# Context attention: queries projected in two parts behind two score groups, all other array shapes behind the third, and a last key block projected with 96 other rows

## The chip, the core and the metric

The kernel runs on one core of a Trainium2 chip. The core has five engines that run their own instruction queues in order: TensorE (PE, with a weight-load half PEld), VectorE (DVE), ScalarE (ACT), GpSimd (POOL) and SyncE (SP), whose queue issues nearly all DMAs here. They wait for each other through semaphores. The metric is the device time of one execution in microseconds (us); the time of a kernel is the median of several executions.

## What is computed

One transformer block in float32 on x of shape (2, 1024, 256), with a context of shape (2, 154, 192): self attention, attention to the context, and a gated feed-forward, each behind a layer norm and with a residual.

```python
def _attention(xq, xkv, wq, wk, wv, wo, bo):        # 16 heads of 64
    q = (xq @ wq).reshape(B, S, N_HEADS, D_HEAD)
    k = (xkv @ wk).reshape(B, T, N_HEADS, D_HEAD)
    v = (xkv @ wv).reshape(B, T, N_HEADS, D_HEAD)
    attn = softmax(einsum('bihd,bjhd->bhij', q, k) * D_HEAD ** -0.5, axis=-1)
    return einsum('bhij,bjhd->bihd', attn, v).reshape(B, S, D_ATTN) @ wo + bo

x = _attention(h1, h1, sa_wq, sa_wk, sa_wv, sa_wo, sa_bo) + x        # h1 = layernorm(x)
x = _attention(h2, cond_emb, ca_wq, ca_wk, ca_wv, ca_wo, ca_bo) + x  # h2 = layernorm(x), 154 keys
a, gate = split(layernorm(x) @ ff_w1 + ff_b1)
x = a * gelu(gate) @ ff_w2 + ff_b2 + x
```

## The kernel before

Work is cut into 16 *units*: 2 batches times 8 pairs of heads (128 columns of the projections). The program is written out by hand in order (`manual_schedule`): each engine runs its instructions in the order in which the Python code emits them, and the framework adds the semaphore waits. Three stages follow each other: self attention (about 0 to 719 us), context attention (about 719 to 948) and feed-forward (to the end).

*Self attention* has 128 steps `p` of two score tiles each (L465). VectorE takes the row maxima (L626), ScalarE the exponentials (L476), and four small DMAs exchange the halves' statistics (`exchange`, L486). One step later `join` (L490 to L503) computes a correction: POOL forms `dd`, ScalarE `ee` (L498), POOL `zz` and `den`; VectorE a reciprocal `rd` (L573), POOL scales the exponentials (L577). Two steps later VectorE transposes them into pT (L591), and TensorE sums with the values into `po` (`self_values`, L512). Beside that the next unit's projections run from the list `work`. A list `later` holds loads, one of which is issued a step.

*Context attention* has three score groups a unit (`CG`: 3, 3 and 2 row tiles of 128 queries), 48 groups `c` in all. I call them the unit's first, second and third group or position. For a group, `cross_first` issues the scores `sc` (L754, array shape 64x128, 154 columns a matmul) and the maxima (L759); its `then` issues the exponentials (L770); `late`, run in the next group, the reciprocal `rden` (L778) and POOL's scaling (L781). `cross_drain` transposes the group before that into a ring (L797). `cross_regroup` copies ring blocks between partitions with DMAs on SP (L814). `cross_values` sums probabilities and values into `poc` (L833, shape 64x64), in two parts a unit that VectorE evicts (L846).

Beside the groups run the next unit's projections: queries `pq_ca` (L348, in two row tiles, evicted by ScalarE at L363), keys `pk_ca` (L701, evicted at L705), and for every second unit values `pv_ca` (L717, 128 rows and then 32 rows, evicted at L726 and L727 and spread over partitions by DMAs at L729 and L734). Also the output projections `py` (L443, 128x128, added to x by VectorE at L450) from the list `outs`, and the steps of the layer norms from the list `side` (POOL or ScalarE normalise at L253 or L256, TensorE turns at L266, ScalarE evicts at L281).

A projection's closure writes matmuls when it is called, and returns the eviction, which waits in the list `stores` until `flush(stores)`. In the loop over `c` that call comes behind the scores of the next group and ahead of its exponentials. So ScalarE sees: exponentials of group c, evictions of what was projected beside group c, exponentials of group c + 1.

PSUM is divided into three pools: two score tiles of two banks (`ps_s`), two banks `mm` (`mm_tile`) and two banks `po` (`sum_tile`). `two_banks` takes both mm banks, as the queries do. Bank pools rotate, and a new tile waits until its bank's earlier reader is done.

In before the order of a unit's groups on TensorE is: scores, queries (512 columns, all at once); scores, first part of the context sums of an earlier unit, keys, one output; scores, second part of the sums, values or an output, output. `run_work` (L536) decides what is taken, by the number of free mm banks.

The parts of that, and of the loops, that the change edits:

Of the kernel before, what the change touches and what calls it, by code (L numbers as in the profile page):

```python
# [13 lines left out]
P = 128  # L14
# [4 lines left out]
def tile_transformer_block(ctx: ExitStack, tc: tile.TileContext, a: dict, out: bass.AP):  # L19
# [182 lines left out]
    spare = {"bank": mm_tile, "out": mm_tile, "keys": mm_tile}  # L202
# [436 lines left out]
    def self_beside(ui):  # L639

        parts = 2 if 0 < ui < HP else 1
        nxt = self_pieces(*units[ui + 1], parts) if ui + 1 < NU else cross_pieces(*units[0], KB)
# [31 lines left out]
    def self_drain(p):  # L674

        if joins:
            drain.append(scale_groups(*joins.pop(0)))
        if SA < p <= SA + LAG:
            turn_groups(p - LAG - 1)

# [5 lines left out]
    def cross_pieces(b, pr, m=P):  # L686

        t = {}

        def q():  # L690
            t["q"] = p2.tile([P, S], F32, tag="QT", name=f"q_ca{b}_{pr}")
            t["k"] = p2.tile([P, S], F32, tag="KT", name=f"k_ca{b}_{pr}")
            qk["ca", b, pr] = (t["q"], t["k"])
            pq = two_banks(f"pq_ca{b}_{pr}")
            project_both(pq, wsl["ca", pr, "q"], hT["ca", b], m)
            return lambda: take_both(t["q"], pq, scale)

        def keys():
            pk = spare["keys"](f"pk_ca{b}_{pr}")
            for c in range(2):  # L700
                nc.tensor.matmul(  # L701
                    pk[:, :T], lhsT=wsl["ca", pr, "k"][:, c, :],
                    rhs=ctxT[:, c, b * TP:b * TP + T], start=(c == 0), stop=(c == 1),
                )
            return lambda: nc.scalar.copy(t["k"][:, :T], pk[:, :T])  # L705

        def values():

            v = vs["ca", b, pr // 2] = pt_.tile([P, NM + 2, VC], F32, tag="V", name=f"v_ca{b}_{pr}")
            nc.vector.memset(v[:, NM:, :], 0.0)
            pv = mm_tile(f"pv_ca{b}_{pr}")
            for n, rows_ in ((0, P), (1, KB)):
                for c in range(2):
                    nc.tensor.matmul(  # L717
                        pv[:rows_, n * VC:(n + 1) * VC],
                        lhsT=ctxT[:, c, b * TP + n * P:b * TP + n * P + rows_],
                        rhs=wsl["ca", pr, "v"][:, c, :], start=(c == 0), stop=(c == 1),  # L720
                    )

            def store():
                for n in range(NM):
                    own = slice(n * QG, (n + 1) * QG)
                    nc.scalar.copy(v[own, n, :], pv[own, :VC])  # L726
                nc.scalar.copy(v[:KB, NM, :], pv[:KB, VC:])  # L727
                later.insert(0, lambda: [
                    nc.sync.dma_start(  # L729
                        out=v[(1 - n) * QG:(2 - n) * QG, n, :], in_=v[n * QG:(n + 1) * QG, n, :])  # L730
                    for n in range(NM)
                ])
                later.insert(1, lambda: [
                    nc.sync.dma_start(out=v[a4 * KB:(a4 + 1) * KB, NM + a4 % 2, :], in_=v[:KB, NM, :])  # L734
                    for a4 in range(1, P // KB)
                ])

            return store

        pieces = [costing(2, q), costing(1, keys)]  # L740
        return pieces + ([costing(1, values)] if pr % 2 == 0 else [])

# [60 lines left out]
    def cross_regroup(c):  # L803

        for a2 in range(2):
            ui, n = divmod(c - len(CG) - 2 - a2, len(CG))
            if n != 0 or not 0 <= ui < NU:
                continue
# [8 lines left out]
    def cross_values(ui, a2):  # L817
# [9 lines left out]
        po = {a4: sum_tile(f"poc_{ui}_{a4}") for a4 in quarters}  # L827
# [24 lines left out]
    def cross_beside(ui):  # L852

        if ui + 1 < NU:
            for what in "kv" if ui else "":
                load_weights("ca", units[ui + 1][1], what)
            pieces = cross_pieces(*units[ui + 1])
            work.extend(pieces[:2])
            held.extend(pieces[2:])
        if ui == 3:  # L860
            norm_beside("ca", B - 1)
        if ui > HP + 1:
            ob, oh = divmod((ui - HP - 2) // HP, 2)
            t0 = ((ui - HP - 2) % HP) * 2
            out_pieces("ca", ob, oh, (t0, t0 + 1))
        if ui == NPAIR + HP + 1:
            norm_beside("ff", 0)
# [7 lines left out]
    def cross_weigh(c):  # L875

        for part in range(2):
            ui, n = divmod(c - len(CG) - 4 - part, len(CG))
            if n == 0 and 0 <= ui < NU:
                run(lambda: cross_values(ui, part))  # L880

# [83 lines left out]
    with tc.manual_schedule():  # L965
# [39 lines left out]
        copies()  # L1005
        copies = turn[3]()
        part("k", 1)
# [10 lines left out]
        later.append(tiles[0])  # L1018
        later.append(lambda: load_weights("sa", units[1][1], "v"))
        later.extend(tiles[1:] + chunks)  # L1020
# [5 lines left out]
        for p in range(SA):  # L1026
            if p % (2 * SH) == 0:
                self_beside(p // (2 * SH))
            if p == SA - SH:
                work.extend(held)  # L1030
                held.clear()
            then = self_first(p)
# [17 lines left out]
        for c in range(CA):  # L1050
# [16 lines left out]
            elif c % len(CG) == 1 and 1 <= c // len(CG) < NU - 2:  # L1067
                load_weights("ca", units[c // len(CG) + 2][1], "q")
            if c % len(CG) == len(CG) - 1:
                work.extend(held)  # L1070
                held.clear()
            flush(adds)
            then = cross_first(c)
            flush(stores)
# [79 lines left out]
```

## Time and profile before

| | |
|---|---|
| median of 3 executions | 1148.21 us (1148.07 to 1151.43) |
| the profiled execution's own time | 1148.76 us |
| its span | 1147.0 us |
| instructions | 36735 |
| DMA | 59.94 MB, q1 (SP's queue) busy 20.8% of the 16 engines' span |

Busy time of the engines by stretches of the span, in us. TensorE's granted clock is 1.00 in all of them:

| stretch | length | TensorE | weight loads | VectorE | ScalarE | POOL |
|---|---|---|---|---|---|---|
| 0 to 50, opening | 50 | 42.05 | 26.49 | 30.83 | 27.88 | 22.16 |
| 50 to 700, self attention | 650 | 641.80 | 332.56 | 585.99 | 428.97 | 491.78 |
| 700 to 740, crossing | 40 | 35.30 | 18.95 | 32.46 | 25.29 | 30.06 |
| 740 to 800, context | 60 | 58.92 | 39.23 | 36.23 | 34.09 | 36.34 |
| 800 to 900, context | 100 | 99.81 | 64.19 | 61.18 | 59.40 | 50.56 |
| 900 to 960, context and first gates | 60 | 58.94 | 42.39 | 39.55 | 35.81 | 34.00 |
| 960 to 1147, feed-forward | 187 | 183.47 | 158.44 | 46.76 | 37.20 | 9.06 |

A row is read against its length: what TensorE's busy time lacks to it is idle time of TensorE. "Busy" counts a matmul from its start to its modelled end. The chain of waits, which the next part shows, goes back from the last instruction to what released it, step by step, and gives the start, the length and the engine, tile and line of each stretch of work; "x12" there counts instructions, of which the profile shows two for each float32 matmul of the program.

### The profile page before, as it was taken

What the parts mean: (1) busy time and instruction counts of PE and PEld (TensorE: products, weight loads), DVE (VectorE), ACT (ScalarE), POOL (GpSimd) and SP (SyncE); (2) the same over time, 40 slices, a digit from 0 to 9 for tenths busy, and PEclk for the clock granted to TensorE, in tenths of its full rate; (3) what the DMA queues carried; (4) which work ended last, traced back from release to release, by engine and by line L of the source; (5) the groups of instructions that cost most, each with busy time, mean ns of one, the idle gap of its engine ahead of it and who ended that gap; (6) DMA issues with size and microseconds to landing.
All of it is one profiled execution on the core that took longest, in us unless ns stands there. A gap on an engine that the chain in (4) does not pass through costs nothing.

```text
span 1147.0 us, 36735 instructions
## 1 busy us (share of the span) xinstructions
PE 1120.3 (98%) x14372; PEld 682.2 (59%) x14372; DVE 833.0 (73%) x1183; ACT 648.6 (57%) x2082; POOL 674.0 (59%) x1568
## 2 busy tenths in 40 slices
PE   8899999999999999999999999999999999999998
PEld 6444444545545545545545554566666667888887
DVE  4888899898898999999899989647666664222222
ACT  4666667666765665676666665637655571041111
POOL 2777777778777777777777777738644453020000
PEclk9999999999999999999999999999999999999999
DMA  2222112101111111111111110267554442000000
GB/s 80 68 71 66 35 32 46 41 13 40 33 29 40 31 31 44 31 31 40 31 31 40 25 28 12 52 141 208 144 120 117 116 88 56 10 10 10 19 10 19
DMA packets 104910, 59.94 MB, mean 52 GB/s; under 512 B 32090, under 2 KB 95522, under 8 KB 104738
## 3 DMA queue, kind: packets, MB, share of 16 engines
q1 hardware_dynamic: 103506, 56.93, 20.8%
q8 instruction: 114, 1.87, 0.7%
q10 hardware_dynamic: 1232, 0.66, 0.2%
q14 instruction: 58, 0.48, 0.1%
HBM read 27.91 MB, written 2.10 MB: 26 GB/s over the span
## 4 chain that ended last, share of the span: by engine, by line
PE 80%; ACT 6%; DMA 3%; DVE 3%; POOL 3%; SPq 2%; issue 2%; DVEq 0%; ACTq 0%; POOLq 0%
PE po L512 15%; PE s L465 15%; PE pa L920 10%; PE py_sa L443 5%; PE py_ca L443 5%; PE pf L943 5%; PE pq_ca L348 5%; ACT p L476 4%; PE pv_sa L379 4%; PE poc L833 4%; PE pk_sa L348 3%; PE pq_sa L348 3%; PE sc L754 3%; DMA st<-st 2%; SPq L486 2%; DVE st L626 2%
## 5 line engine op out<-in xcount | busy, mean ns | idle before, releaser
L476 ACT ACTIVATE p<-s,st 128x512 f32<-128x512 f32 x512 | 345.2, 686 | 203.2 <-DVE st L626 191.5
L577 POOL TENSOR_SCALAR p<-p,rd,ee 128x512 f32<-128x512 f32 x512 | 386.4, 771 | 44.8 <-DVE rd L573 43.9
L626 DVE TENSOR_REDUCE st<-s 128x2 f32<-128x1024 f32 x256 | 301.3, 1218 | 32.9 <-PE s L465 20.1
L591 DVE STREAM_TRANSPOSE pT<-p 128x1024 f32<-128x1024 f32 x256 | 302.1, 1218 | 0.0
L465 PE MATMUL s<-k_sa,q_sa 64*32 64x512 f32 x4096 | 252.1, 594 | 13.5 <-ACT p L476 12.8
L512 PE MATMUL po<-pT,v_sa 64*64 64x256 f32 x4096 | 235.8, 379 | 0.0
L512 PEld LDWEIGHTS po<-pT,v_sa 64*64 64x64 f32 x4096 | 150.4, 133 | 109.1 <-issue 32.8
L781 POOL TENSOR_SCALAR p<-p,rden 128x154 f32<-128x154 f32 x256 | 97.0, 401 | 98.5 <-DVE rden L778 98.0
L465 PEld LDWEIGHTS s<-k_sa,q_sa 64*32 64x32 f32 x4096 | 65.3, 106 | 137.4 <-issue 69.3
L770 ACT ACTIVATE p<-sc,neg 128x154 f32<-128x154 f32 x256 | 96.1, 396 | 79.8 <-DVE rden L778 78.1
L929 DVE SCALAR_TENSOR_TENSOR u<-pa,cols,gate 128x256 f32<-128x256 f32 x64 | 31.0, 484 | 124.4 <-ACT gate L926 124.4
L920 PE MATMUL pa<-hT_ln,wf 128*128 128x256 f32 x512 | 121.0, 379 | 0.0
L926 ACT ACTIVATE gate<-pa,cols 128x256 f32<-128x256 f32 x64 | 30.3, 474 | 151.5 <-PE pa L920 151.5
L920 PEld LDWEIGHTS pa<-hT_ln,wf 128*128 128x128 f32 x512 | 96.8, 190 | 13.7 <-DVE u L929 0.4
L476 ACT ACTIVATION_READ_ACCUMULATOR p<-s,st 128x1 f32 x512 | 103.6, 202 | 0.0
L759 DVE TENSOR_REDUCE neg<-sc 128x6 f32<-128x924 f32 (+1 forms) x48 | 48.4, 1010 | 43.1 <-PE sc L754 43.1
L379 PEld LDWEIGHTS pv_sa<-sa_wv,hT_ln 64*128 64x128 f32 x1024 | 59.3, 188 | 18.7 <-DMA st<-st 9.2
L500 POOL TENSOR_TENSOR zz<-ee,st 128x8 f32<-128x8 f32 x128 | 25.9, 203 | 67.5 <-ACT ee L498 67.5
L943 PE MATMUL pf<-wf,u 128*128 128x256 f32 x256 | 65.0, 379 | 0.2 <-DVE u L929 0.2
L379 PE MATMUL pv_sa<-sa_wv,hT_ln 64*128 64x128 f32 x1024 | 63.3, 276 | 1.7 <-DMA sa_wv<-in_L_xattn_sa_wv_dram 1.4
L443 PE MATMUL py_ca<-ca_wo,o_ca 128*128 128x256 f32 x256 | 60.8, 384 | 0.3 <-ACT hT_ln L281 0.3
L348 PE MATMUL pq_ca<-hT_ln,ca_wq 64*128 64x512 f32 (+1 forms) x304 | 60.5, 591 | 0.2 <-ACT hT_ln L281 0.2
(87 smaller groups left out, 1243.6 us busy)
## 6 DMA issues: line engine op xcount, KB each, us to landing
wf<-pT_ca SPq DMA_DIRECT2D x128, 128.0 KB, 2.4
st<-st SPq DMA_DIRECT2D x512, 1.0 KB, 1.8
v_sa<-v_sa SPq DMA_DIRECT2D x32, 256.0 KB, 3.5
sa_wq<-in_L_xattn_sa_wq_dram SPq DMA_DIRECT2D x32, 128.0 KB, 2.9
sa_wk<-in_L_xattn_sa_wk_dram SPq DMA_DIRECT2D x32, 128.0 KB, 2.8
sa_wv<-in_L_xattn_sa_wv_dram SPq DMA_DIRECT2D x32, 128.0 KB, 3.0
ca_wq<-in_L_xattn_ca_wq_dram SPq DMA_DIRECT2D x32, 128.0 KB, 3.1
wf<-in_L_xattn_ff_w_dram SPq DMA_DIRECT2D x12, 256.0 KB, 3.7
```

Of the source, the lines that this page charges most:

```text
L348: nc.tensor.matmul(pq[r][f:f + m, at:at + n], lhsT=wt[own, c, f:f + m], rhs=h[own, c, t0:t0 + n], start=(c == 0), stop=(c == NH - 1), tile ...
L379: nc.tensor.matmul(pv[r][:, i * P:(i + 1) * P], lhsT=h[own, c, i * P:(i + 1) * P], rhs=wt[own, c, :], start=(c == 0), stop=(c == NH - 1), ...
L443: nc.tensor.matmul(py[:, :D], lhsT=o[:, i, t * P:(t + 1) * P], rhs=wo[kind][:, half * HP + i, :], start=(i == 0), stop=(i == HP - 1),)
L465: nc.tensor.matmul(sc[a4 * KB:(a4 + 1) * KB, j, :], lhsT=q[r, c:c + KB], rhs=k[r, h * HB:(h + 1) * HB], start=True, stop=True, tile_positi ...
L476: nc.scalar.activation(pr[:, j, :], sc[:, j, :], AF.Exp, bias=st[:, 0, 0, i, j:j + 1], accum_out=st[:, 0, 1, i, j:j + 1],)
L512: nc.tensor.matmul(po[a2][j * DH:(j + 1) * DH, :QH // 2], lhsT=v[r, t, e, j * DH:(j + 1) * DH], rhs=pT[r, j * NK + n, :], start=(t == 0 an ...
L577: nc.gpsimd.tensor_scalar(pr[:, j, :], pr[:, j, :], rd[:, c:c + 1], ee[:, 0, c:c + 1], op0=ALU.mult, op1=ALU.mult,)
L591: nc.vector.transpose(halves[h][:, :, c:c + KB], groups.pop(0).rearrange("p j (n k) -> p (j n) k", k=KB))
L626: nc.vector.tensor_reduce(st[:, 0, 0, i, :], sc[i], AX.X, ALU.max, negate=True)
L781: nc.gpsimd.tensor_scalar(pr_[:, j, i, :T], pr_[:, j, i, :T], rden[:, j, i:i + 1], 1.0, op0=ALU.mult, op1=ALU.mult,)
L920: nc.tensor.matmul(pa[:, half, :TF * P], lhsT=w1[:, c, half * DF + f * P:half * DF + (f + 1) * P], rhs=h[:, c, t0 * P:(t0 + TF) * P], star ...
L943: nc.tensor.matmul(sums[blk][i][:, :D], lhsT=sums[blk, "u"][:, f, i * P:(i + 1) * P], rhs=w2[:, f, :], start=(f == 0), stop=(f == NF - 1),)
```

## The change

- *Queries.* `cross_queries` takes a start `t0` and a width `n`. Unit 1's queries are still projected in one go. For units 2 to 15 two calls of 256 columns a row half are made, behind the scores of the first and the second group of the unit before; each call takes both mm banks.
- *The rest of a unit* stands behind the third group's scores: both parts of the context sums, the second part now in mm banks, then the keys (in a `po` bank), an output or a norm step, every second time the values, and an output. Behind the first two groups stand only: the last self-attention sums (unit 1), two outputs as long as more than two wait (unit 2), or one norm step. `norm_beside` for batch 1 begins a unit earlier.
- *Values.* The last key block is projected with the 96 keys ahead of it as 128 rows, and only the last 32 rows are copied, on partitions 96 to 127; from there DMAs spread it to the other three.
- *DMAs.* `cross_regroup` issues its eight DMAs in one group (before: four in each of two groups), and in the main loop comes last ahead of `later`.
- *Crossing.* The last `join` of self attention runs at group 1 instead of 0, behind the scaling and exponentials of the context; the last two `turn_groups` run at groups 1 and 3 (before: 1 and 2), ahead of `flush(drain)` and `flush(lates)`.
- *Opening.* The second part of the first keys is projected before the last rows are turned, and the values weights of unit 1 are loaded at step 3, ahead of that step's scores, not from `later` behind its exchange.

```diff
+    def cross_queries(b, pr, m=P, t0=0, n=S // 2):
+        if t0 == 0:
+            qk["ca", b, pr] = (
+                p2.tile([P, S], F32, tag="QT", name=f"q_ca{b}_{pr}"),
+                p2.tile([P, S], F32, tag="KT", name=f"k_ca{b}_{pr}"),
+            )
+        pq = two_banks(f"pq_ca{b}_{pr}_{t0}")
+        project_both(pq, wsl["ca", pr, "q"], hT["ca", b], m, t0, n)
+        return lambda: take_both(qk["ca", b, pr][0], pq, scale, t0, n)
...
+    def context_values(b, pr):
...
-            for n, rows_ in ((0, P), (1, KB)):
+        for n, k0 in enumerate((0, TP - P)):
             for c in range(2):
...
+                    pv[:, n * VC:(n + 1) * VC], lhsT=ctxT[:, c, b * TP + k0:b * TP + k0 + P],
+                    rhs=wsl["ca", pr, "v"][:, c, :], start=(c == 0), stop=(c == 1),
+                )
+        last = P // KB - 1
...
+            nc.scalar.copy(v[last * KB:, NM + last % 2, :], pv[last * KB:, VC:])
...
     def cross_regroup(c):
+        ui, n = divmod(c - len(CG) - 2, len(CG))
+        if n != 0 or not 0 <= ui < NU:
+            return
         for a2 in range(2):
-            ui, n = divmod(c - len(CG) - 2 - a2, len(CG))
-            if n != 0 or not 0 <= ui < NU:
-                continue
...
-        po = {a4: sum_tile(f"poc_{ui}_{a4}") for a4 in quarters}
+        po = {a4: (mm_tile if a2 else sum_tile)(f"poc_{ui}_{a4}") for a4 in quarters}
...
     def cross_weigh(c):
-        for part in range(2):
-            ui, n = divmod(c - len(CG) - 4 - part, len(CG))
-            if n == 0 and 0 <= ui < NU:
+        ui, n = divmod(c - 2 * len(CG) - 2, len(CG))
+        if n == 0 and 0 <= ui < NU:
+            for part in range(2):
                 run(lambda: cross_values(ui, part))
+            flush(stores)
...
-        copies = turn[3]()
         part("k", 1)
+        copies = turn[3]()
...
+            if p == LAG + 1:
+                load_weights("sa", units[1][1], "v")
             then = self_first(p)
...
             then = cross_first(c)
             flush(stores)
+            if c == 1:
+                turn_groups(SA - 2)
+            elif c == LAG + 1:
+                turn_groups(SA - 1)
             flush(drain)
             flush(lates)
             lates.append(then())
-            if c <= SH:
-                self_drain(SA + c)
-            cross_regroup(c)
-            cross_drain(c)
-            cross_weigh(c)
-            flush(stores)
-            if c == 1:
-                spare["keys"] = sum_tile
-                run_work(3, 0)
-                spare["keys"] = mm_tile
-            elif c > 1:
-                run_work(2, 1, n_sum=2 * (SH < c < 2 * NPAIR and c % len(CG) == 0))
-            if SH - LAG < c <= SH:
-                run(lambda: self_values(2 * NU - 1, c - SH + LAG - 1))
+            if c == 1:
+                drain.append(scale_groups(*joins.pop(0)))
+            if n < len(CG) - 1:
+                cross_drain(c)
+            if ui == 0:
+                if n == 1:
+                    run(lambda: cross_queries(*nxt))
+                    run(lambda: cross_keys(*nxt, sum_tile))
+            elif n < len(CG) - 1:
+                if nxt:
+                    run(lambda: cross_queries(*nxt, t0=n * S // 4, n=S // 4))
+                if c <= SH:
+                    run(lambda: self_values(2 * NU - 1, n))
+                elif len(outs) > 2:
+                    run_work(0, 1, None, 2)
+                else:
+                    run_work(0, 1, sum_tile)
+            else:
+                cross_weigh(c)
+                if nxt:
+                    run(lambda: cross_keys(*nxt, sum_tile))
+                run_work(0, 1, None, 1)
+                if nxt and nxt[1] % 2 == 0:
+                    run(lambda: context_values(*nxt))
+                flush(stores)
+                spare["out"] = mm_tile
+                if outs:
+                    run(outs.pop(0))
+            if n == len(CG) - 1:
+                cross_drain(c)
+            cross_regroup(c)
```

## The prediction

> **What bounds the kernel now.** I read the page first, then the chain of waits over the context attention, then each engine's timeline there.
>
> ```profile
> PE 1120.3 (98%) x14372; PEld 682.2 (59%) x14372; DVE 833.0 (73%) x1183; ACT 648.6 (57%) x2082; POOL 674.0 (59%) x1568
> PEclk9999999999999999999999999999999999999999
> PE 80%; ACT 6%; DMA 3%; DVE 3%; POOL 3%; SPq 2%; issue 2%; DVEq 0%; ACTq 0%; POOLq 0%
> ```
>
> TensorE is busy 98% of 1147.0 us at full clock, so at most 26.7 us are idle. A gain must come from those or from shorter TensorE work; any new wait of TensorE adds to the end. One unit of the chain (start, length, work), in the period 849.62 to 864.87:
>
> ```profile
> 849.62 0.99 PE sc L754 x12
> 850.60 3.43 PE pq_ca L348 x16
> 854.03 0.79 PE sc L754 x12
> 854.82 1.46 PE poc L833 x24
> 856.28 0.72 PE pk_ca L701 x4
> 857.00 1.73 PE py_ca L443 x8
> 858.73 0.72 PE sc L754 x8
> 859.45 1.46 PE poc L833 x24
> 860.90 2.04 PE pv_ca L717 x8
> 862.95 1.92 PE py_ca L443 x8
> ```
>
> It is TensorE from end to end: 15.25 us with a values projection, 13.22 us without (836.40 to 849.62). The same scores cost 0.99 behind another array shape (128x128) and 0.79 behind their own (64x128); outputs 1.92 behind the values, 1.73 behind the keys. So a change of shape costs some 0.2.
>
> **What the change saves.** (1) Shape changes. A unit without values goes from six to three: by columns streamed, pq gives 3.43 us for 8 pairs of 512, twice over two passes, 0.84 ns a column. At that pace 13.22 holds some 12.1 us of streaming, leaving 1.1 for six changes, 0.18 each; three fewer are 0.55. With values it goes from eight (the 32-row block counts as a shape) to three: 5 x 0.18 = 0.9. Units 6, 8, 10, 12, 14 give 5 x 0.55 = 2.75, units 7, 9, 11, 13 give 4 x 0.9 = 3.6. Counted through the instruction orders of both kernels, units 1 to 5 lose nine changes, 1.6. Sum 7.9. Projecting 96 more rows streams the same columns, so only the shape change is gained there.
>
> (2) The opening. The unit-1 values weights are queued on SP behind the fourth statistics exchange, and TensorE waits 0.40 and 0.97 for them. In the change they go one exchange earlier, behind the x tile that issued at 37.74, and would land near 42, well before 46.7: 1.37 gained. Turning the last rows after k's second part covers a 0.19 wait. Sum 1.56.
>
> (3) Waits of the layer norms and evictions in 740:960: 1.1 + 0.4 + 0.4 + 0.3 + 0.2 = 2.4. The norms move one unit earlier; I take these waits as gone (bound 0 to 2.4). All savings: 11.9.
>
> **What it costs: the second half of the queries.** Both halves use the two banks of the mm pool (L338, L341). The second half may start only when ScalarE has copied the first out, and those copies stand on ScalarE behind the six exponentials of the first score group (L770); the copies are stored after the next group's scores are issued. The rows, VectorE and ScalarE of the same unit:
>
> ```profile
> 850.65 1.12 DVE L759 TENSOR_REDUCE neg<-sc 128x6 f32<-128x924 f32 x1 [0.57 <-PE sc L754]
> ```
>
> ```profile
> 851.89 0.39 ACT L770 ACTIVATE p<-sc,neg 128x154 f32<-128x154 f32 x1 [3.09 <-DVE rden L778]
> ...
> 854.09 1.11 ACT L363 ACTIVATE q_ca<-pq_ca 128x512 f32<-128x512 f32 x2
> ```
>
> From the scores' end (850.60): first exponential at +1.29, query copies at 854.09 = +3.49. For 256 columns I take the opening's copies (q_sa, 128x256): 0.38 for one, 0.67 for two. Banks are free at +3.87 and +4.16. TensorE wants them after half a projection (1.73) and twelve scores (0.79): +2.52. Wait 1.35 to 1.64. Before, 3.43 of queries, 0.79 of scores and 1.46 of another pool's banks lay there, and hid the copies. A restart costs up to 0.27 (scores after a 2.29 wait took 1.06, not 0.79). So 1.35 to 1.91 a unit; I take 1.8, as both banks are needed and a weight load lies ahead. ScalarE is in order: behind the copies queue the next group's exponentials, but their lateness is absorbed by the third position, where the 2.8 us of context sums use sum banks first. There the order is scores, context sums, keys, outputs and values; the key copy has 3.5 us of outputs as cover.
>
> Filler decides which units pay. Units 1 and 2 have self-attention values (3.6) or two outputs (3.5) behind the half: no wait. Units 5 to 13 have nothing: 9 x 1.8 = 16.2. Units 3 and 4 have only a norm turn (0.44 and a change of shape): 1.1 each. In unit 4 no output or values follow the keys, so the key copy is bare: TensorE ends the keys near +10.8, ScalarE, with 1.39 of norm evictions in each of two slots, copies them near +11.6: 0.9. Unit 14 also has norm activations (two, 0.97, waiting for VectorE's offset) ahead of its query copies: 2.0. Unit 15 has no queries, only two turns; the second waits for a normalisation behind the first exponentials: 3.49 + 0.97 against TensorE at 1.6, 2.9 less 0.3 that today's unit 15 waits: 2.6. Sum 23.9.
>
> **The crossing from self attention.**
>
> ```profile
> 728.51 1.06 PE L754 MATMUL sc<-k_ca,q_ca 64*128 64x154 f32 x12 [2.29 <-ACT k_ca L705]
> ```
>
> Today TensorE waits 2.29 there. The change puts VectorE's two transposes (2.3) ahead of rden, and the last join on POOL behind the first context scaling (2.27, L781). From today's rows: POOL's scaling ends 723.9, transposes 725.1, rden 725.3, context scaling 727.6, dd 728.4, so ScalarE's ee (L498) runs at 728.4 instead of 724.87; behind it queue unit 1's query copies (1.0) and key copy (0.3). Scores start near 729.9: +1.4. Then the last group's scaling (four, 3.02) can start only at 729.45 and its transposes end near 734.5, while TensorE asks for them at 732.75 for L512 (today they ended at 731.2 and L512 began at 733.00): +1.8. Together 3.2, bounded by 0 (if TensorE finds both in time) and 4.5.
>
> DMAs: the eight regroup transfers (L814) now go out together, after the third position, on SP. Four took 2.5 us and landed 2.4 later; the next context sums are a unit away (13 us), and the weight loads queued behind them have half a unit. Only in the feed-forward, where slots are 1.73, do eight come close: 0.5.
>
> **Two rules of the Trainium skill, beside the rows.** The halves are 16 instructions of 256 columns where 8 pairs had 512. The opening's query projection of just that form (64x256 x16) ran from 20.32 to 22.25, 1.93 with one shape change, so no extra.
> The skill's "TensorEngine Tiling (Array Packing)", Instruction Overhead, speaks against the split: about 60 cycles for each matmul. By an estimate from it, 16 more instructions a unit over 14 units at 25 ns would be 5.6 us; the row shows none, and I take none.
> The windowed clock was 1.00 over 700:740, the 2.29 wait included.
> "TensorE: Matmul & The Clock Gate", HAM oscillation, warns of TensorE gaps over some 3.4 us, after which it runs at half clock; a crossing wait of 3.7 would be just such a gap, and by the page could cost a further 2 or so. No row here has so long a gap.
>
> **The sum.** 23.9 + 3.2 + 0.5 - 11.9 = +15.7. The profiled run's own time was 1148.76 (span 1147.0 and 1.8 around it), 0.55 over the median of 1148.21; set on the median, 1163.9. I say 1163.
>
> **Rivals.**
> *The second half's banks come free in time (faster).* For it: ScalarE is only 57% busy and no wait of this kind is in today's trace. Against: a chain of 3.87 measured us against 2.52 of cover. Were it so in all units, 16.2 + 2.2 + 2.0 go and 1163.9 becomes 1143.5. It decides from a wait under 0.1 a unit, where savings and the other costs cancel. 8%.
> *Half the wait* (a copy starts earlier, the turns or the slower first passes fill more, the crossing costs nothing): 9 x 0.9 less and 3.2 less, some 1152. Against: ScalarE's queue is in order. 14%.
> *More waits than I count* (half clock after the crossing, regroup transfers late for the sums each unit, norms on POOL late): 0.6 more in 14 units, 1172. Against: DMA has a whole unit. 8%.
> *The order doesn't change as said:* the instruction order shows the halves and their wait on ScalarE. 0%.
>
> **Numbers.** My forecast, 70%: waits 1.35 to 1.91, crossing 1.4 to 4.5, turns at half to full, norm waits gone or not: 1155 to 1171. Low end stretched to 1152 for the half-wait case. About 0.3%, 3.4 us, is what measurement tells from no change. Faster beyond it 7%, same 7%, slower 86%.
>
> **What would show it.** TensorE waits on ScalarE's q_ca copies once in each of units 5 to 13, 1.4 to 1.9 long; units of 14.5 and 16.2 us instead of 13.2 and 15.3; scores of the second and third position at 0.79 and 0.52 with no shape change; no wait for sa_wv; 3 to 4 us at the crossing. Wrong, if those units are shorter than before: then a bank came free earlier than its copy's place in the queue says.

## The result and the profile after

| | median of the runs | ratio to the kernel before (95% interval) | span of the profiled run | mean granted clock |
|---|---|---|---|---|
| before | 1148.43 us (6 runs) | 1 | 1147.0 | 1.000 |
| changed | 1180.62 us (6 runs, 1177.98 to 1181.95) | 1.0273 [1.0258, 1.0288] | 1180.2 | 0.991 |

The change made the kernel 2.7% slower, 32 us. The direction was forecast, the size was not: 1163 in a range of 1155 to 1171. The first rows of the page of the changed kernel, its clock row, and the engines' row of its chain of waits:

```profile
PE 1128.7 (96%) x14596; PEld 718.5 (61%) x14596; DVE 837.8 (71%) x1183; ACT 649.5 (55%) x2110; POOL 672.8 (57%) x1568
PEclk9999999999999999999999999999999989999999
PE 77%; ACT 9%; DMA 3%; DVE 3%; issue 3%; SPq 2%; POOL 2%; DVEq 0%; POOLq 0%; ACTq 0%
```

TensorE's busy time rose by 8.4 us (1120.3 before) and its idle time by 24.8 (26.7 before, 51.5 now). The clock row, flat before, has an 8, and the chain runs through ScalarE for 9% instead of 6%. The table of TensorE's waits (waiting operation, what it waited for, us in total, times, longest) names the idle time; the second and the last of the rows below were not foreseen:

```profile
PE pq_ca L348 <- ACT q_ca L363: 14.6, 11, 1.6
PE poc L829 <- ACT hT_ln L281: 5.8, 4, 1.7
PE sc L750 <- ACT k_ca L697: 3.9, 2, 3.5
PE ph_ln L266 <- ACT xn_ln L256: 2.5, 1, 2.5
PE pv_sa L379 <- ACT k_sa L371: 1.6, 1, 1.6
```

A unit in the middle (833.00 to 849.38, with values) in TensorE's timeline: start, length, operation, and in brackets the idle time ahead of it and its releaser.

```profile
833.00 1.06 PE L750 MATMUL sc<-k_ca,q_ca 64*128 64x154 f32 x12
833.89 1.89 PE L348 MATMUL pq_ca<-hT_ln,ca_wq 64*128 64x256 f32 x16
835.62 0.95 PE L750 MATMUL sc<-k_ca,q_ca 64*128 64x154 f32 x12
838.00 2.05 PE L348 MATMUL pq_ca<-hT_ln,ca_wq 64*128 64x256 f32 x15 [1.43 <-ACT q_ca L363]
...
849.38 0.79 PE L750 MATMUL sc<-k_ca,q_ca 64*128 64x154 f32 x8
```

The unit takes 16.38, its neighbour without values 14.64 (849.38 to 864.02); 16.2 and 14.5 were forecast. ScalarE's timeline beside it shows the queue: the last exponential of the first group, then the two copies, then the second group.

```profile
837.18 0.41 ACT L766 ACTIVATE p<-sc,neg 128x154 f32<-128x154 f32 x1
837.45 0.23 ACT L766 ACTIVATION_READ_ACCUMULATOR p<-sc,neg 128x1 f32 x1
837.54 0.68 ACT L363 ACTIVATE q_ca<-pq_ca 128x256 f32<-128x256 f32 x2
838.07 0.43 ACT L766 ACTIVATE p<-sc,neg 128x154 f32<-128x154 f32 x1
```

So the steady units do what was forecast. Where the rest went is told by the starts of the units in both traces (scores of a unit's first group; the feed-forward from its first gates):

| from | start before | start after | shift added up to there |
|---|---|---|---|
| unit 0 | 719.50 | 721.99 | +2.49 |
| unit 1 | 728.51 | 732.23 | +3.72 |
| unit 6 | 806.56 | 818.36 | +11.80 |
| unit 14 | 921.74 | 942.41 | +20.67 |
| feed-forward | 947.98 | 981.33 | +33.35 |
| end of the span | 1147.0 | 1180.2 | +33.2 |

Units 6 to 13 added 8.87. Units 14 and 15 added 12.68 by themselves, where 2.95 were forecast. Two things are at work there that the sum did not have.

*Context sums wait for a norm turn.* TensorE's timeline at the end of unit 14, then ScalarE's over the same time:

```profile
950.60 0.66 PE L266 MATMUL ph_ln<-ident,xn_ln 128*128 128x128 f32 x4
951.18 0.79 PE L750 MATMUL sc<-k_ca,q_ca 64*128 64x154 f32 x8
951.91 0.65 PE L829 MATMUL poc<-wf,v_ca 64*64 64x256 f32 x4
954.24 1.55 PE L829 MATMUL poc<-wf,v_ca 64*64 64x256 f32 x10 [1.68 <-ACT hT_ln L281]
```

```profile
952.58 0.69 ACT L363 ACTIVATE q_ca<-pq_ca 128x256 f32<-128x256 f32 x2
953.10 1.08 ACT L281 ACTIVATE hT_ln<-ph_ln,cols 128x256 f32<-128x256 f32 x2
```

The turn `ph_ln` at 950.60 takes a `po` bank. Its eviction is on ScalarE behind the second group's exponentials and the query copies and ends at 954.18. The context sums want that bank 0.8 us of scores later. It is the query copies' mechanism on another pool. Units 3, 4 and 14 wait 1.68 each, unit 15 0.76.

*The clock halves.* TensorE's clock was granted at half in four intervals, together 20.5 us, at 97.3, 732.1, 954.0 and 967.7. A table by windows shows two of them and the stretch before each (columns: length, then busy time of PE, PEld, DVE, ACT, POOL with their instructions, the granted clock, DMA share, GB/s):

```profile
728.70:732.10 3.40, 0.01 (x2) 0.00 (x0) 1.28 (x4) 1.41 (x7) 2.58 (x11) 1.00 0.52 159
732.10:735.50 3.40, 3.27 (x20) 3.02 (x22) 2.20 (x4) 1.67 (x10) 3.40 (x6) 0.51 0.06 17
...
950.60:954.00 3.40, 1.96 (x17) 1.17 (x16) 0.90 (x2) 3.40 (x13) 1.87 (x5) 1.00 0.00 0
954.00:957.40 3.40, 3.17 (x32) 1.90 (x36) 0.71 (x2) 1.66 (x9) 1.36 (x5) 0.50 0.20 43
```

In the first stretch TensorE waits 3.52 for unit 1's keys; in the third it waits 1.68, and not once for longer. Each is followed by 3.4 us at half clock, in which TensorE does about half its work while it looks busy: an instruction of the context sums takes 0.63 us behind 954.24 and 0.38 at full clock. So its busy time can grow though it changes shape less often. Half of 20.5 us, 10.2, bounds what this cost.

### The profile page after: what moved, and what is told of

It is laid out like the page before. It is cut to its first block, busy times and chain, and to the rows that moved or that the text cites. A ratio compares the mean times of both kernels' runs of the same rounds, so it can differ in the third digit from the quotient of the medians.

```text
span 1180.2 us, 37220 instructions
## 1 busy us (share of the span) xinstructions
PE 1128.7 (96%) x14596; PEld 718.5 (61%) x14596; DVE 837.8 (71%) x1183; ACT 649.5 (55%) x2110; POOL 672.8 (57%) x1568
## 4 chain that ended last, share of the span: by engine, by line
PE 77%; ACT 9%; DMA 3%; DVE 3%; issue 3%; SPq 2%; POOL 2%; DVEq 0%; POOLq 0%; ACTq 0%
PE po L512 16%; PE s L465 15%; PE pa L914 9%; PE py_sa L443 5%; PE py_ca L443 5%; PE pf L937 5%; PE poc L829 4%; ACT p L476 4%; PE pk_sa L348 4%; PE pv_sa L379 4%; PE pq_sa L348 3%; ACT p L766 3%; DMA st<-st 3%; PE pq_ca L348 2%; SPq L486 2%
## 5 line engine op out<-in xcount | busy, mean ns | idle before, releaser
L626 DVE TENSOR_REDUCE st<-s 128x2 f32<-128x1024 f32 x256 | 301.3, 1218 | 32.6 <-PE s L465 20.5
L465 PE MATMUL s<-k_sa,q_sa 64*32 64x512 f32 x4096 | 253.9, 596 | 13.4 <-ACT p L476 12.7
L512 PE MATMUL po<-pT,v_sa 64*64 64x256 f32 x4096 | 236.5, 380 | 1.1 <-DVE rden L774 1.1
L512 PEld LDWEIGHTS po<-pT,v_sa 64*64 64x64 f32 x4096 | 151.1, 133 | 110.9 <-issue 31.7
L348 PE MATMUL pq_ca<-hT_ln,ca_wq 64*128 64x256 f32 (+2 forms) x528 | 66.5, 417 | 14.7 <-ACT q_ca L363 14.6
L348 PEld LDWEIGHTS pq_ca<-hT_ln,ca_wq 64*128 64x128 f32 (+1 forms) x528 | 49.8, 180 | 24.0 <-ACT q_ca L363 17.5
```

The costliest lines, as they stand in the source:

```text
L348: nc.tensor.matmul(pq[r][f:f + m, at:at + n], lhsT=wt[own, c, f:f + m], rhs=h[own, c, t0:t0 + n], start=(c == 0), stop=(c == NH - 1), tile ...
L465: nc.tensor.matmul(sc[a4 * KB:(a4 + 1) * KB, j, :], lhsT=q[r, c:c + KB], rhs=k[r, h * HB:(h + 1) * HB], start=True, stop=True, tile_positi ...
L512: nc.tensor.matmul(po[a2][j * DH:(j + 1) * DH, :QH // 2], lhsT=v[r, t, e, j * DH:(j + 1) * DH], rhs=pT[r, j * NK + n, :], start=(t == 0 an ...
L626: nc.vector.tensor_reduce(st[:, 0, 0, i, :], sc[i], AX.X, ALU.max, negate=True)
```

## The experiments

Each ran beside the kernel before on the same chip. Since the time of that kernel differed from one such group to the next (medians of 1148.3 to 1152.9), ratios and places in the trace are compared, not bare times. "c" counts score groups, `n` is the position in a unit. The theory after the result: the split costs what was forecast, and the rest comes from banks whose evictions stand in a late queue and from the half clock that such waits bring. The rivals: that the split itself costs more than its wait, that the clock halves by itself in this order, that the crossing or the opening holds the loss.

### Whole queries behind the first group

```diff
-                if nxt:
-                    run(lambda: cross_queries(*nxt, t0=n * S // 4, n=S // 4))
+                if nxt and n == 0:
+                    run(lambda: cross_queries(*nxt))
```

> The changed kernel with the queries of units 2 to 15 projected in one piece of 512 columns again, behind the first score group; nothing stands behind the second but the norm steps and outputs; the third position is as in the change. Theory 1 (the second half waits for its two banks, behind the exponentials on ScalarE): the waits of TensorE for q_ca (11, 14.6 us) and their restarts vanish, units 8 and 9 go from 14.6 and 16.4 us to some 12.8 and 14.5, and the time falls by 16 to 20 to about 1162. Rival 1 (the split itself costs, by more instructions): the same time, so this run alone doesn't tell these two apart. Rival 2 (the third position, with both parts of the context sums in one go, is what costs): units stay at 14.6 and 16.4, and the time within 3 us of 1180.6.

1175.43 us, ratio 1.0228 [1.0207, 1.0249]. The wait for q_ca is gone, as forecast, but not the time: a steady unit takes 13.65 and 15.38 instead of 14.64 and 16.37, a gain of 1.0 of the 1.8. A new wait took its place, of the keys for VectorE's evictions of the context sums:

```profile
856.43 0.61 PE L829 MATMUL poc<-pT_ca,v_ca 64*64 64x256 f32 x8
857.97 0.79 PE L693 MATMUL pk_ca<-ctxT,ca_wk 96*128 96x154 f32 x4 [0.93 <-DVE o_ca L842]
858.60 3.62 PE L443 MATMUL py_ca<-ca_wo,o_ca 128*128 128x256 f32 x16
```

The context sums' wait for norm turns grew from 5.8 to 10.6 us, and the clock stood at half for 23.9 us. So the time fell by some 5 us, not by the 16 to 20 expected: undoing the split alone did not show its price, because other waits took its place.

### The halves in two pools

```diff
-        pq = two_banks(f"pq_ca{b}_{pr}_{t0}")
+        pq = [bank(f"pq_ca{b}_{pr}_{t0}_{r}") for r in range(2)]
...
+                    run(lambda: cross_queries(
+                        *nxt, t0=n * S // 4, n=S // 4, bank=sum_tile if first else mm_tile))
```

(`first`: position 0 from unit 3 on; the norm turn behind that half takes an mm bank.)

> The changed kernel with as many halves and instructions, but from unit 3 on the first half of the queries goes into the two po banks and only the second into the mm banks (a norm turn behind the first half then takes an mm bank). Theory 1 (bank reuse): the second half starts without a wait; the second part of the context sums then waits for the second half's copies, some 0.6 to 0.9, so about 1 us a unit is gained, 8 to 12 us in all: 1169 to 1173. Rival 1 (the split's instructions): no gain, 1179 to 1182.

1172.38 us, ratio 1.0209 [1.0183, 1.0234], with as many instructions as the changed kernel. The split stays, and the steady wait of 1.43 becomes 0.51 (units of 13.67 and 15.40): it was the bank, not the form of the matmuls.

```profile
834.40 1.89 PE L348 MATMUL pq_ca<-hT_ln,ca_wq 64*128 64x256 f32 x16
838.78 1.14 PE L829 MATMUL poc<-wf,v_ca 64*64 64x256 f32 x14 [0.51 <-ACT q_ca L363]
```

The second half now starts with no wait. The 0.51 is the second part of the context sums, which finds the second half's mm banks not yet copied out. From a unit's first scores to its context sums these halves take 5.75 (831.00 to 836.75), whole queries in the run ahead of this 5.73 (848.49 to 854.22): the split by itself costs next to nothing. Here too the wait was in part passed on: three times the queries now wait for a norm turn's eviction from an mm bank (`hT_ln`), 6.2 us in all.

### Norm turns in the third position only

```diff
-                    run_work(0, 1, sum_tile)
+                    run_work(0, 1)
...
-                run_work(0, 1, None, 1)
+                flush(stores)
+                run_work(0, 1, sum_tile, 1)
```

> The changed kernel with the norm turns moved from behind the first two score groups to the third position, behind the keys, in a po bank; the steps without a turn stay. Theory 2 (a turn's po bank is evicted late by ScalarE, so the context sums wait, and close waits bring the half clock): the four waits of the context sums for hT (5.8 us) and the one of a turn for its normalised rows (2.5) vanish, and with them the half clock near 954 to 957 and 968 to 978, another 6 us: 1164 to 1168, granted clock mean 0.996 or more. Rival 3 (the half clock comes by itself, whatever the waits): some 8 us, 1172 to 1173, clock mean still 0.991.

1169.25 us, ratio 1.0172 [1.0148, 1.0197]: 1.0 points of the 2.7 with these lines alone. No wait of the context sums for hT is left; at the end of unit 14 they follow the scores at once:

```profile
942.18 0.83 PE L750 MATMUL sc<-k_ca,q_ca 64*128 64x154 f32 x7
942.93 1.09 PE L829 MATMUL poc<-wf,v_ca 64*64 64x256 f32 x16
```

The clock stands at half for 6.8 us instead of 20.5 (mean 0.997), and the steady units and their 1.43 are as in the changed kernel. TensorE's busy time is back at 1120.2 us. The rival that kept the clock at 0.991 without these waits falls. Part of the gain is given back later: two turns now stand behind the first gates, and from there to the end it takes 202.5 instead of 198.8.

### The crossing as before

```diff
+    def self_drain(p):
+        if joins:
+            drain.append(scale_groups(*joins.pop(0)))
+        if SA < p <= SA + LAG:
+            turn_groups(p - LAG - 1)
...
-            if c == 1:
-                turn_groups(SA - 2)
-            elif c == LAG + 1:
-                turn_groups(SA - 1)
...
-            if c == 1:
-                drain.append(scale_groups(*joins.pop(0)))
+            if c <= SH:
+                self_drain(SA + c)
```

> The changed kernel with the crossing as it was: the last join at group 0, the last two turns of groups at groups 1 and 2 behind the scaling. Theory (the crossing's order costs, and its 3.5 us wait brings a half-clock window): the wait for k_ca falls from 3.5 to about 2.3, that of the self-attention sums for the transposes from 1.1 to 0, the half clock near 732 goes (1.6): together 3 to 5 us, 1176 to 1178. Rival 4 (the crossing was late only because self attention ended 2.5 later): no change beyond 1 us.

1179.15 us, ratio 1.026 [1.0236, 1.0284]; the interval overlaps the changed kernel's. Its trace shows the mechanism: unit 1's scores wait 2.39 for k_ca instead of 3.52, and L512 no longer waits 1.10 for VectorE. The 3.4 us at half clock stay: in the stretch of 3.4 us before them TensorE is busy for 0.30 of the time.

### The opening as before

```diff
-        part("k", 1)
         copies = turn[3]()
+        part("k", 1)
...
-        later.extend(tiles + chunks)
+        later.append(tiles[0])
+        later.append(lambda: load_weights("sa", units[1][1], "v"))
+        later.extend(tiles[1:] + chunks)
...
-            if p == LAG + 1:
-                load_weights("sa", units[1][1], "v")
```

> The opening as before (last rows turned ahead of k's second part; unit 1's values weights loaded from the list behind the exchange), the rest as changed. Theory 1 (the opening's edits gained nothing: the values of step 5 wait 1.60 for ScalarE's k_sa eviction instead of 1.37 for the weights, and the self stage's pace hides the rest): within 1.5 us of the changed kernel's 1180.6, TensorE waits for sa_wv again and the self stage ends within 1 us of the changed kernel's. Rival (the opening gains 1.56 as I predicted): 1.5 slower, about 1182. Second rival (the opening's order itself causes the wait and half clock near 94 to 101 us): 1178, no half clock there, the self stage 2 us shorter.

1181.89 us, ratio 1.0261 [1.0243, 1.0279], no difference that can be told. The wait for sa_wv (0.53 and 0.87) is back, and context attention starts at 721.57 (changed kernel 721.99). This line of the changed kernel shows what had taken its place:

```profile
47.49 4.32 PE L379 MATMUL pv_sa<-sa_wv,hT_ln 64*128 64x128 f32 x64 [1.60 <-ACT k_sa L371]
```

The weights are in time, but the projection waits longer (1.60 against 0.40 and 0.97 before) for ScalarE to copy the keys out of an mm bank.

### The last key block with 32 rows again

```diff
-        for n, k0 in enumerate((0, TP - P)):
+        for n, rows_ in ((0, P), (1, KB)):
```

(with the copy and the DMAs that spread it, as before the change)

> The last key block of the values is projected with 32 rows again instead of 128; all else as changed. Theory 1 (a change of shape inside the values, 0.2 to 0.3 for each of 7 or 8 projections, all of them on TensorE's path): 1.4 to 2.5 us slower than the changed kernel, units with values 16.6 to 16.7 instead of 16.37, those without unchanged. Rival (the wait for the query banks or other waits swallow it, or the fewer rows cost nothing): within 0.5 us.

1183.61 us, ratio 1.0273 [1.0256, 1.0289]. Whole runs can't tell it from the changed kernel; the trace can: a unit with values takes 16.69 (865.40 to 882.09) instead of 16.37, one without 14.65. So projecting 32 rows instead of 128 costs 0.32 more, some 2.5 over eight projections: theory 1, seen in the units alone.

### Three parts undone together

```diff
+                if nxt and n == 0:
+                    run(lambda: cross_queries(*nxt))
...
-                    run_work(0, 1, sum_tile)
+                    run_work(0, 1)
...
+                flush(stores)
+                run_work(0, 1, sum_tile, 1)
```

(and the crossing's lines as shown above, and `n == 0` for `n == 1` in unit 0)

> Three parts undone together: whole queries behind the first group, norm turns only in the third position, the crossing's join and turns where they were; also unit 1's queries and keys behind unit 0's first group instead of its second. Theory 1 (the parts are separate: the split costs about 1.8 a unit of which a new wait of the keys for VectorE's evictions gives back 0.92, the turns' bank and the half clock that its waits bring 11, the crossing 1.5): 1156 to 1161, steady units 13.65 and 15.38, keys wait 0.92 for the context sums' evictions in some 12 units, half clock at most near 731 and 956. Rival (half clock comes by itself in this order): 1165 or more with clock below 0.995 though the waits for norm evictions and query copies are gone.

1157.82 us, ratio 1.0054 [1.0034, 1.0073]; clock 0.997. This kernel is called c1 below. Units of 13.65 and 15.38, the keys wait 0.92 in 12 units (11.0 in all), the clock halves twice, for 6.8 us. The three parts are not simply separate: alone, their runs gain 0.5, 1.0 and 0.1 points of ratio, together 2.2, of which the new place of unit 1's projections may have a share. The crossing is not quite that of before: unit 1's scores wait 3.1 there, by the trace for VectorE's transposes (`pT`), where before they waited 2.3 for the keys. What is left is still slower than before; the next runs ask what the keys' wait is made of.

### The keys elsewhere

Behind the second group, from unit 2 on (with unit 1 in it the order deadlocks, so it has no time):

```diff
+                elif nxt and ui > 1:
+                    run(lambda: cross_keys(*nxt, sum_tile))
```

> As c1 (whole queries, norm turns in the third position, the crossing's order as before), and from the third unit on the keys go from the third position, where they take a bank that the context sums have just filled, to behind the second group's scores. Theory 1 (c1's 0.92 a unit is the price of that bank's reuse): no wait of the keys from unit 2 on, units 12.7 and 14.5, 10 to 11 us less than c1: a ratio of 0.995 to 0.998 to the kernel before. Rival (the next wait in the third position, or ScalarE's queue, takes it back): units 13.4 or more and a ratio of 1.002 to 1.006.

1189.62 us, ratio 1.0349 [1.0332, 1.0366]: slower than the changed kernel. The keys' own wait became one of the context sums, for the bank that the keys now hold:

```profile
778.55 0.80 PE L757 MATMUL sc<-k_ca,q_ca 64*128 64x154 f32 x8
779.27 0.65 PE L836 MATMUL poc<-wf,v_ca 64*64 64x256 f32 x4
781.75 0.87 PE L836 MATMUL poc<-wf,v_ca 64*64 64x256 f32 x10 [1.82 <-ACT k_ca L704]
```

The copy of the keys stands behind the second group's exponentials, just where the norm turns' evictions stood. Ten such waits cost 17.8 us, three waits for the keys' weights 4.9, and the clock halves in eleven intervals, 37.5 us. The same, with the last unit's two outputs behind its first two groups:

```diff
+                if not nxt:
+                    run(outs.pop(0))
```

> As the run before it, and in the last unit, which has no queries of a next one, its two outputs stand behind the first two score groups instead of the third. Theory 1 (the 2.87 that the third scores of c1's last unit wait for exponentials, and the half clock that follows a 3.41 us stretch in which TensorE was busy for less than half, go when those two groups have work): 4 to 5 us less than the run before it, no half clock near 945. Rival (VectorE's adds of the outputs delay the transposes, and the wait moves to the third position's sums or into the feed-forward): within 1.5 us of it.

1188.09 us, ratio 1.0338 [1.0324, 1.0353], about 1.5 us less, not 4 to 5. The last unit itself gains 4.0 (13.75 to 9.79), but between the first gates a turn now waits 1.21 instead of 0.64 and the clock halves at 990. And behind the queries, from unit 3 on, with the keys' weights loaded a position earlier:

```diff
+                    if ui > 1 and len(outs) <= 2:
+                        run(lambda: cross_keys(*nxt, sum_tile))
+                        keyed.add(ui)
...
+            if n == 2 and ui + 2 < NU:
+                load_weights("ca", units[ui + 2][1], "k")
```

> As c1, and from the fourth unit on the keys follow the queries directly behind the first group, in a po bank, so that ScalarE copies them ahead of the second group's exponentials; their weights are loaded a position earlier than their unit; the last unit's two outputs stand behind its first two groups. Theory 1 (a bank costs nothing when its copy stands ahead of the exponentials, and 0.92 or 1.8 when it is wanted while the copy or eviction is queued): no wait of TensorE on k_ca or o_ca in units 3 to 14, units 12.7 and 14.5, some 10 us less there than c1 and 2.9 or more in the last unit: a ratio of 0.991 to 0.996 to the kernel before, clock at least 0.997. Rival (the keys' weights come late, or the second group's exponentials, now behind one more copy, stop the third scores): units of 13.4 or more and a ratio of 1.000 or over.

1159.21 us, ratio 1.0095 [1.008, 1.0109]. The theory holds for the copy (no wait on k_ca) and fails for the wait on o_ca: what now stands behind the context sums waits in the keys' place, nearly as long.

```profile
847.79 0.61 PE L836 MATMUL poc<-pT_ca,v_ca 64*64 64x256 f32 x8
849.33 3.72 PE L443 MATMUL py_ca<-ca_wo,o_ca 128*128 128x256 f32 x16 [0.93 <-DVE o_ca L849]
```

With one more change of shape between queries and scores the units take 14.05 and 15.77. So it is not the keys' place that matters, but when VectorE evicts.

### Evictions ahead of the reciprocal

VectorE's timeline in the kernel with three parts undone, at a third position:

```profile
858.20 0.76 DVE L762 TENSOR_REDUCE neg<-sc 128x4 f32<-128x616 f32 x1
859.88 0.19 DVE L781 RECIPROCAL rden<-den 128x6 f32<-128x6 f32 x1 [0.92 <-ACT p L773]
859.99 1.38 DVE L849 COPY o_ca<-poc 128x256 f32<-128x256 f32 x4
```

VectorE idles 0.92 at the second group's reciprocal, until ScalarE has done that group's last exponential; the evictions are queued behind it, though the sums' first part ended at 858.2.

```diff
             then = cross_first(c)
             flush(stores)
+            if n == len(CG) - 1:
+                cross_weigh(c)
...
-                cross_weigh(c)
```

(and the last unit's outputs as above)

> As c1, with the context sums and their evictions written ahead of the second group's reciprocal in the third position, and the last unit's two outputs behind its first two groups. In c1 VectorE stands at that reciprocal (rden at 859.88) for the last exponentials of the second group, 0.92, and the four evictions of the context sums are queued behind it; so do the keys. Theory (the 0.92 is VectorE's queue, not the bank alone): no wait on o_ca in the units, 12.7 and 14.5 long, 10 to 11 us less than c1, and 3 to 4.5 less in the last unit: a ratio of 0.991 to 0.995 to the kernel before. Rival (the reciprocal 1.4 later makes POOL's scaling and the transposes late, and the wait moves there): units of 13.4 or more, a ratio of 0.999 or over.

1148.6 us, ratio 0.9986 [0.9975, 0.9997]; this kernel is called c5. The units are what the theory said, 12.66 and 14.38 (848.52 to 862.90), and VectorE no longer idles there:

```profile
855.76 0.76 DVE L762 TENSOR_REDUCE neg<-sc 128x4 f32<-128x616 f32 x1
856.44 1.41 DVE L849 COPY o_ca<-poc 128x256 f32<-128x256 f32 x4
857.77 0.18 DVE L781 RECIPROCAL rden<-den 128x6 f32<-128x6 f32 x1
```

The total falls short of the expected 0.991 to 0.995: from the first gates to the end it takes 204.8, the kernel before 199.0. Two norm turns had been pushed behind them.

```diff
-                    run_work(0, 1)
+                    run_work(0, 1, sum_tile if n == 0 and ui >= NU - 2 else None)
```

> As c5, and the first groups of the last two units may take a norm turn too (in a po bank, whose eviction stands ahead of the second group's exponentials), so that the four turns of the feed-forward's first norm are done ahead of it. In c5 the attention's units end 6 us earlier than before, but two turns stand between the first gates, TensorE waits 1.27 and 0.72 for them and the clock halves near 951: from the first gate to the end c5 takes 204.8, the kernel before 199.0. Theory (c5's gain is lost to these): no wait for xn_ln or hT_ln behind the first gate, 199 to 201 from there to the end, 3 to 5 us less than c5, a ratio of 0.994 to 0.997 to the kernel before. Rival (the turns' wait for the normalisation comes back inside the last unit, as in the changed kernel): within 1.5 us of c5, with a wait of over 1 for xn_ln ahead of the first gate.

1144.31 us, ratio 0.9957 [0.994, 0.9974]: faster than both kernels, by 0.4% and, by the two ratios, 3.1%. The feed-forward starts at 946.53 with all turns behind it and takes 198.9; no wait for xn_ln or hT_ln is left there.

```profile
936.30 1.06 PE L757 MATMUL sc<-k_ca,q_ca 64*128 64x154 f32 x12
939.12 0.60 PE L266 MATMUL ph_ln<-ident,xn_ln 128*128 128x128 f32 x4
...
946.03 0.66 PE L266 MATMUL ph_ln<-ident,xn_ln 128*128 128x128 f32 x4
946.53 1.89 PE L921 MATMUL pa<-hT_ln,wf 128*128 128x256 f32 x8
```

Its span, 1145.4, holds 10.2 us at half clock, two of the three intervals in self attention, which this kernel leaves as in the changed one, and the third at the crossing. It keeps of the change the third position's grouping, the values' 128 rows and the opening; it has whole queries.

## Why the prediction was right in sign and too small

Its terms, put into the stages of the table of starts, against what was measured:

| stage | forecast | measured | what made the difference |
|---|---|---|---|
| to unit 0 (opening) | -1.6 | +2.5 | gain absent, 1.6; half clock at 97.3, up to 1.7; 0.8 open |
| unit 0 (k_ca) | +1.4 | +1.2 | |
| units 1 to 5 | +3.8 | +8.1 | half clock at 732.1, up to 1.7; sums waiting for hT in units 3 and 4, 3.4 |
| units 6 to 13 | +8.6 | +8.9 | |
| units 14 and 15 | +3.0 | +12.7 | half clock, up to 6.8; sums waiting for hT, 2.4 |
| feed-forward | +0.5 | -0.2 | |
| sum | +15.7 | +33.2 | |

- *The second half's wait*: right in its mechanism and nearly in its size. The forecast of 1.35 to 1.91 took in the restart; 1.43 is the wait alone, and the unit's 14.64 against 12.66 with whole queries and no wait (c5) puts it at 1.98 with the restart. 11 waits named q_ca. The copies' place in ScalarE's queue, read from the rows of before, gave it. The two-pool halves showed that it is the bank.
- *Shape changes*: right in size as far as the runs separate it. With whole queries and no wait a unit took 12.66 and 14.38, against 13.22 and 15.25 before: 0.56 and 0.87 gained, 0.55 and 0.9 forecast.
- *ScalarE's lateness "is absorbed by the third position, where the 2.8 us of context sums use sum banks first"*: this step failed. It took the sum banks to be free. In units 3, 4, 14 and 15 a norm turn, which the sum counted as 0.44 of filler, had just taken one, and its eviction stands in the same late queue. That cost 5.8 us of waits, and most of the half clock came with them: without those turns the ratio fell to 1.0172 and the half clock from 20.5 to 6.8 us.
- *The clock*: this step failed too. The crossing's 3.7 was seen as a risk of "a further 2 or so" and put into a rival of 8%; nothing was counted for shorter waits. Waits of 1.5 to 2.5 halved the clock as well, 20.5 us in all, at most 10.2 lost. One of them is bad luck: the 1.52 ahead of 97.3 stands in the kernel before too, at 94.78, without half clock, and ten of the twelve profiled kernels with the changed opening have none there. Together with the sums' waits (5.8) and the opening's missing 1.6, these come to at most 17.6, and 17.5 us are missing. That they agree so well is partly luck: 10.2 is a bound, 0.8 ahead of unit 0 has no cause found, and the waits for q_ca and k_ca in units 3 to 5 were 2.4 where 4.9 was forecast.
- *The crossing*: 3.2 forecast. The run with the old order shows 1.13 less of the k_ca wait and 1.10 less of the L512 wait, 2.2 together, by its trace; its whole time can't tell it from the changed kernel.
- *The opening*: 1.56 forecast, no gain that can be told. TensorE was 0.84 ahead at the first scores (17.60 against 18.44), 0.46 at 51.74, and by 74 us it was behind. With the changed opening context attention started between 719.37 and 723.42 in the profiled runs, with the old one at 719.50 and 721.57, so one run alone can't show 1.56. The weights were early, but the projection's bank was not free.
- *Norm waits of 2.4 gone*: right for those waits: between 740 us and the feed-forward TensorE's only waits for norms are the context sums' 5.8 for hT and one of 2.5 for xn_ln, in unit 15, which was foreseen. The turns now cost elsewhere: it is their banks that the context sums wait for.
- The rival "more waits than I count" is nearest to what happened, at 1180 instead of its 1172, but of its three causes only the half clock came, and mostly in other places than the crossing: no wait for the regroup transfers, and none for a norm on POOL, is in the context attention. "Half the wait" and "banks come free in time" fell with the 1.43.

## What to carry to other kernels

When work is regrouped, list each bank or buffer that it takes, and for each the place of its eviction in an in-order queue: whatever is emitted behind a group's exponentials comes late, whether it is the copy that the change is about, a filler's eviction, or VectorE's, stuck behind an operand that ScalarE has yet to make. Moving the waiting instruction passed the wait to the next taker: the whole queries, the keys behind the second group and the keys behind the queries each showed it. Moving the eviction ahead in its queue removed it. And where several waits fall close together, count the clock too: here it lost up to 10.2 us, against 5.8 of waits that had not been counted.

## What was not expected of the hardware

The half-clock intervals begin on a grid of 3.413 us and last one, two or three steps of it. I cut all 14 profiled executions into that grid (in the kernel before, which has no such interval, counted from where its record of the clock begins), and sorted the stretches at full clock, without the first 10 us, by the share in which TensorE was busy:

| busy share of a stretch | stretches | next one at half clock |
|---|---|---|
| below 0.45 | 29 | 29 |
| 0.45 to 0.50 | 17 | 13 |
| 0.50 to 0.61 | 79 | 10 |
| 0.61 and more | some 4500 | 3 |

So below a half it was nearly sure, and just above it sometimes. What counted was not one long gap but the sum of waits that fell into one stretch, and where the grid happened to lie: the kernel before has a 2.29 us wait at its crossing that is split over two stretches (0.68 and 0.65 busy) and loses nothing. With the grid's place differing between executions, the same wait costs in one and not in another: in the changed kernel the context sums' 1.68 is followed by half clock in unit 14 and not in units 3 and 4.

The Trainium skill's "TensorE: Matmul & The Clock Gate", HAM oscillation, has the rule that gaps over some 3.4 us bring the half clock; the length of the window agrees with the grid, the rule for a gap does not with the 1.68 us above. The same page's section on a second failure mode says that frequent short idles between groups of matmuls can do it too; that is nearer to what these runs show, and the share of a half is what they add.
